# A state-space scan and window attention in one kernel: a column-grouped convolution, and the scan's products in two slots a tile

## The chip, the cores and the metric

The kernel runs on one core of one Trainium2 chip. The metric is the device time of one execution in microseconds (us), as the median of several runs. TensorE (PE) does matrix products, VectorE (DVE) and ScalarE (ACT) elementwise work, GpSimd (POOL) elementwise work on SBUF, and SyncE (SP) issues DMAs; ACT issues some too. All data are 32-bit floats.

## The reference, cut to what matters

The input is 8 images of 192 channels, 64 x 64. Layer 0 is a two-dimensional selective scan, layer 1 window attention with an MLP.

```python
# layer 0
x = conv1x1(x, W_in)                                  # 192 -> 384 channels
x = conv3x3_depthwise(x, W_dw) + b_dw                 # one 3 x 3 filter per channel
p = conv1x1(x, W_xd)                                  # 16 channels
ws, Ls, Us, Ds = (conv1x1(p, w) for w in (W_w, W_l, W_u, W_d))
xs = [x, x.T, flip(x), flip(x.T)]                     # four directions
Gl, Gm, Gr = ws / (|Gl| + |Gm| + |Gr| + eps)
for step in range(8):                                 # within chunks of 8 columns
    h = L * x + Gl * shift_up(h) + Gm * h + Gr * shift_down(h)
out = h * U + xs * D
y = sum over directions (w_m[d] * out[d])
y = conv1x1(grn(layernorm2d(y)), W_out)               # 384 -> 192
# layer 1
s = layer_norm(y as tokens)
q, k, v = s @ qkv_w.T                                 # windows of 8 x 8, 6 heads of 32
attn = l2n(q) @ l2n(k).T * temperature
attn = softmax(keep the 16 largest of each row + bias)
x2 = s + (attn @ v) @ proj_w.T
out = x2 + gelu(layer_norm(x2) @ fc1.T) @ fc2.T
```

## The kernel before

Three streams work on three images at once. `front` makes the convolved input of image b+1, `scan` runs the scan of image b, `windows` does the attention and MLP of image b-1. `side_by_side` (L716) takes a step of whichever stream is furthest behind its share; the build's scheduler then fixes one static order for each engine. Each engine takes its instructions in that order, so an instruction that waits holds all behind it on the same engine. The first front runs alone, and so do the last image's windows.

*Front (L208).* For each of 3 groups of 128 channels and each of 8 strips of 8 rows: SP loads the strip (`xt`), two products with `w_in` make `pin` (L223), ACT copies it to one of three padded strips `xin`, with two more small copies for the rows that neighbouring strips share (L226 to L232). The 3 x 3 filter is then nine products of a 128 x 128 diagonal matrix (`diag`, loaded from DRAM per channel group) with a shifted view of the strip, summed in PSUM (L242). ACT reads the sum twice, in two layouts (`st`, `sn`), and issues both stores (`xs`, `xsT`).

*Scan (L260).* Per image 8 steps t; per step 4 directions x 3 channel groups = 12 tiles of 128 channels x 512 positions; 768 tiles in all, of which 672 have gates (t > 0). `project` (L288) is a product with only 32 rows, rows 32r to 32r+31 of the weights and of `xe` or `xo`, which hold the 16-channel proxy four times over. Per tile, `first` makes the three gates `g` (three PSUM banks, row groups 0 to 2), then `pl` (L, row group 3), which DVE multiplies with the input `xv` to `lx` (L319); then D, which DVE multiplies to `dx` (L323); `second`, called one tile later, makes U, which DVE multiplies with the new state to `hu` (L360). L, D and U take turns in the single bank `u_ps`. The state update runs over ACT (absolute values L330, L331; Ln and Exp L345, L346), POOL (L341, L347, L348, L350) and DVE (L334 or L336 for gates times state, L342, L349, L351, L352). POOL adds the outputs to `y3` (L363 to L371). After 12 tiles `norm` (L373) does the layer norm of the step and stores `z`. `proxy` (L275) prepares the next step's input.

*Windows (L466).* Per image 8 rows of 8 windows: output projection (L494), transposes (L475), q, k, v, the products of the attention, the top-16 search on DVE, softmax (three wide POOL operations, L598, L599, L604), projection, MLP (L678, L679, L689).

PSUM has eight banks: `g_ps` 3, `n_ps` 1 (the denominators `nb`), `u_ps` 1 (L, D, U), `f_ps` 1 (front, proxy, norm), `l_ps` 2 (windows).

Of the kernel before, what the change touches and what calls it, by code (L numbers as in the profile page):

```python
# [17 lines left out]
F32 = mybir.dt.float32  # L18
# [7 lines left out]
P = 128  # L26
# [13 lines left out]
NEG = -100.0  # L40
LN_EXP = "natural_log_exp_and_others"
# [8 lines left out]
def tile_ss2d_then_window_attention(ctx: ExitStack, tc: tile.TileContext, a: dict, out: bass.AP):  # L50
# [31 lines left out]
    w_dw = load("w_dw")  # L82
# [30 lines left out]
    xin = [blank(f"xin{k}", [P, 10, W + 2], 0.0) for k in range(3)]  # L113

    sT, oT, xT = (blank(n, [HALF + 1, 2, GT]) for n in ("sT", "oT", "xT"))
    for t in (sT, oT, xT):
        nc.vector.memset(t[HALF : HALF + 1, 1, :], 1.0)

    dram = ctx.enter_context(tc.tile_pool(name="dram", bufs=2, space=DRAM))
    diag_d = dram.tile([CT, P, 9 * P], F32, name="diag_d", bufs=1)  # L120


    with tc.tile_pool(name="prep", bufs=2) as prep, tc.tile_pool(name="prep_ps", bufs=2, space=PSUM) as prep_ps:
        for ct in range(CT):
            dg = prep.tile([P, 9, P], F32, name="diag")
            for k in range(9):
                nc.vector.tensor_scalar(dg[:, k, :], ident, w_dw[:, ct, k : k + 1], None, ALU.mult)
            nc.sync.dma_start(diag_d[ct], dg.rearrange("p k q -> p (k q)"))

        for d in range(ND):  # L130
            rows = slice(64 * (d // 2), 64 * (d // 2) + 64)
            cols = slice((d % 2) * DIN, (d % 2 + 1) * DIN)
            nc.vector.tensor_scalar(w_g2[rows, cols], w_g2[rows, cols], w_m[rows, d : d + 1], None, ALU.mult)
# [57 lines left out]
    u_ps = ctx.enter_context(tc.tile_pool(name="u_ps", bufs=1, space=PSUM))  # L191
    f_ps = ctx.enter_context(tc.tile_pool(name="f_ps", bufs=1, space=PSUM))
# [15 lines left out]
    def front(b, xs, xsT):  # L208
        xb = x[b].rearrange("(k p) h w -> p k h w", p=HALF)
        n = 0  # L210
        for ct in range(CT):
            diag = fpool.tile([P, 9, P], F32, name="diag")
            nc.sync.dma_start(diag.rearrange("p k q -> p (k q)"), diag_d[ct])
            for s in range(NG + 1):
                if s < NG:

                    prev, cur, nxt = (xin[(n + k) % 3] for k in (-1, 0, 1))
                    n += 1
                    xt = fpool.tile([HALF, 2, 8, W], F32, name="xt")
                    nc.sync.dma_start(xt, xb[:, :, 8 * s : 8 * s + 8, :])  # L220
                    pin = f_ps.tile([P, 8, W], F32, name="fp")
                    for k in range(2):
                        nc.tensor.matmul(  # L223
                            pin, lhsT=w_in[:, k, ct * P : (ct + 1) * P], rhs=xt[:, k], start=k == 0, stop=k == 1
                        )
                    nc.scalar.copy(cur[:, 1:9, 1 : W + 1], pin)  # L226
                    if s == 0:
                        nc.gpsimd.memset(cur[:, 0, :], 0.0)
                    else:
                        nc.scalar.copy(prev[:, 9, 1 : W + 1], pin[:, 0, :])  # L230
                    if s < NG - 1:
                        nc.scalar.copy(nxt[:, 0, 1 : W + 1], pin[:, 7, :])  # L232
                    else:
                        nc.gpsimd.memset(cur[:, 9, :], 0.0)
                    yield
                if s == 0:
                    continue
                strip = xin[(n - (2 if s < NG else 1)) % 3]
                pc = f_ps.tile([P, 8, W], F32, name="fp")
                for k in range(9):  # L240
                    dy, dx = divmod(k, 3)
                    nc.tensor.matmul(  # L242
                        pc, lhsT=diag[:, k, :], rhs=strip[:, dy : dy + 8, dx : dx + W], start=k == 0, stop=k == 8
                    )
                rows = slice((s - 1) * 64, s * 64)
                st = fpool.tile([P, CH, 64], F32, name="st")
                nc.scalar.activation(
                    st.rearrange("p t (i c) -> p i c t", c=CH),
                    pc.rearrange("p i (c t) -> p i c t", t=CH),
                    AF.Identity,  # L250
                    bias=b_dw[:, ct : ct + 1],
                )
                sn = fpool.tile([P, 8, W], F32, name="sn")
                nc.scalar.activation(sn, pc, AF.Identity, bias=b_dw[:, ct : ct + 1])
                nc.scalar.dma_start(xs[:, ct, :, rows], st)
                nc.scalar.dma_start(xsT[:, ct, :, rows], sn)
                yield


    def scan(b, xs, xsT, z, made):  # L260
        gx = small.tile([P, CT, CH], F32, name="gx")

# [12 lines left out]
        def proxy(t):  # L275
# [3 lines left out]
            px = f_ps.tile([P, 512], F32, name="fp")  # L279
# [8 lines left out]
        def project(dst, w, row, col, xp):  # L288
            rows = slice(RG * row, RG * row + RG)
            nc.tensor.matmul(dst, lhsT=w[rows, col : col + P], rhs=xp[rows, :], start=True, stop=True)  # L290

        def first(t, d, ct, xp, x0):
# [14 lines left out]
            if t > 0:  # L307
                g = g_ps.tile([P, 3, 512], F32, name="g")
                for r in range(3):
                    project(g[:, r, :], w_g1, r, ch, xp)  # L310
            pl = u_ps.tile([P, 512], F32, name="pl")
            project(pl, w_g1, 3, ch, xp)
            if t == 0:
                s = hid[d][ct]
                now = by(view(s, [[1, 512]], CH), d) if d % 2 == 0 else state(d, ct)
                nc.vector.tensor_mul(now, by(pl, d), xv)
            else:
                lx = spool.tile([P, 512], F32, name="lx")
                nc.vector.tensor_mul(by(lx, d), by(pl, d), xv)  # L319
            pd = u_ps.tile([P, 512], F32, name="pl")  # L320
            project(pd, w_g2, 2 * (d // 2), (d % 2) * DIN + ct * P, xp)
            dx = spool.tile([P, 512], F32, name="dx", bufs=3)
            nc.vector.tensor_mul(by(dx, d), by(pd, d), xv)  # L323
            if t == 0:
                return dx


            ab = spool.tile([P, 2, 512], F32, name="ab", bufs=1)
            nb = n_ps.tile([P, 512], F32, name="nb")
            nc.scalar.activation(ab, g[:, 0:2, :], AF.Abs)  # L330
            nc.scalar.activation(nb, g[:, 2, :], AF.Abs)  # L331
            pr = spool.tile([P, 3, 512], F32, name="pr")
            if d % 2 == 0:
                nc.vector.tensor_mul(pr, g, view(hid[d][ct], [[CH, 3], [1, 512]]))  # L334
            else:
                nc.vector.tensor_mul(  # L336
                    pr.rearrange("p r (c i) -> p r c i", c=CH),
                    g.rearrange("p r (c i) -> p r c i", c=CH),
                    view(hid[d][ct], [[1, 3], [H + 2, CH], [1, H]]),
                )  # L340
# [12 lines left out]
            return dx  # L353

        def second(t, d, ct, xp, dx, y3):

            pu = u_ps.tile([P, 512], F32, name="pl")
            project(pu, w_g2, 2 * (d // 2) + 1, (d % 2) * DIN + ct * P, xp)
            hu = spool.tile([P, 512], F32, name="hu")
            nc.vector.tensor_mul(like(hu, d), like(pu, d), state(d, ct))  # L360
            yt = y3[:, ct, :]
            if d == 0:
                nc.gpsimd.tensor_add(yt, hu, dx)  # L363
                return
            nc.gpsimd.tensor_add(dx, dx, hu)  # L365
            yt = by(yt, 0)
            if d == 2:

                nc.gpsimd.tensor_add(yt, yt, by(dx, 0))
            else:  # L370
                nc.gpsimd.tensor_add(yt, yt, dx.rearrange("p (c i) -> p i c", c=CH))  # L371

        def norm(t, y3):  # L373
            pm = f_ps.tile([P, 512], F32, name="fp")
# [5 lines left out]
            pv = f_ps.tile([P, NT], F32, name="fp")  # L380
# [17 lines left out]
            ps = f_ps.tile([P, 512], F32, name="fp")  # L398
# [14 lines left out]
        last = None  # L413
        for t in range(CH):
            x0, xe, xo = ready
            y3 = spool.tile([P, CT, 512], F32, name="y3")
            for d in (0, 2, 1, 3):
                for ct in range(CT):
                    xp = xe if d % 2 == 0 else xo
                    dx = first(t, d, ct, xp, x0)  # L420
                    if last:
                        last()
                    last = lambda *args, t=t, d=d, ct=ct, xp=xp, dx=dx, y3=y3: second(t, d, ct, xp, dx, y3)
                    yield
                if d == 1 and t < CH - 1:
                    ready = proxy(t + 1)
            last()
            last = None
            norm(t, y3)
            yield  # L430
# [9 lines left out]
        pg = f_ps.tile([P, 1], F32, name="fp")  # L440
# [16 lines left out]
        pb = f_ps.tile([1, DM], F32, name="fp")  # L457
# [8 lines left out]
    def window_row(b, g, z, wz, bz):  # L466
        def bank(name="lp"):
            return l_ps.tile([P, 512], F32, name=name)
# [272 lines left out]
def _laid_out(i):  # L741
# [8 lines left out]
    w_g1, w_g2 = z(P, ND * DIN), z(P, 2 * DIN)  # L750
# [5 lines left out]
    for r, w in enumerate([f(L0 + "W_d"), f(L0 + "W_u")]):  # L756
        for d2 in range(2):
            at = RG * (2 * d2 + r)
            w_g2[at : at + NS] = w[2 * d2 * DIN : 2 * (d2 + 1) * DIN].T
# [17 lines left out]
        "w_dw": rows(f(L0 + "W_dw").reshape(DIN, 9), P),  # L777
# [40 lines left out]
```

## Time and profile before

| | us | share of the span |
|---|---|---|
| median of 3 runs (13549.14 to 13593.06) | 13569.98 | |
| the profiled execution | 13575.18 | |
| its span | 13573.4 | 100% |
| TensorE busy | 11668.6 | 86% |
| VectorE busy | 6446.2 | 47% |
| GpSimd busy | 6160.8 | 45% |
| ScalarE busy | 4760.2 | 35% |

The mean granted TensorE clock was 0.745 of full speed. Busy times are unions of an engine's instructions. Matmuls are pipelined and their ends are modelled: "2.07 us" for two passes whose successor starts 2.00 us later means 2.00 us of use. Each 32-bit product appears as two passes. In an instruction's line, `32*128 32x512` is 32 rows by 128 columns of the array, with 512 columns streamed through.

### The profile page before, as it was taken

The numbers are of one execution on the slowest core, as the hardware profiler recorded it, in microseconds if no ns is written. First come the engines' busy times: TensorE is split into PE (matmuls) and PEld (weight loads), VectorE is DVE, ScalarE is ACT, GpSimd is POOL, SyncE is SP. The second block draws the span as 40 slices with busy tenths as digits, with TensorE's granted clock in tenths as the row PEclk, the third lists the DMA queues.
The fourth block names the chain that finished last, engine by engine and source line by source line (L and its number), as shares of the span: only waits on it lengthen the run. The fifth ranks groups of instructions, "written<-read, shape, count | busy, mean of one in ns | idle before, by whom it ended". The sixth has DMA issues, their size and how long they took to land.

```text
span 13573.4 us, 124360 instructions
## 1 busy us (share of the span) xinstructions
PE 11668.6 (86%) x44856; PEld 5651.1 (42%) x44856; DVE 6446.2 (47%) x13918; ACT 4760.2 (35%) x8105; POOL 6160.8 (45%) x5590
## 2 busy tenths in 40 slices
PE   7888888889889898988988988898888888878655
PEld 2222344444444444444444444444444444434444
DVE  0355455553555445554455535555455544565222
ACT  1233234333334333433333333443233333333222
POOL 0366445553555434554455435555345534555111
PEclk9667677777777777877777777777777776666777
DMA  3111111111111111111111111111111110000000
GB/s 86 46 50 52 47 36 43 42 39 44 42 38 45 38 40 43 40 42 42 39 41 44 38 43 41 41 43 39 43 41 38 45 34 28 28 24 26 15 11 9
DMA packets 791475, 531.26 MB, mean 39 GB/s; under 512 B 613988, under 2 KB 614567, under 8 KB 790856
## 3 DMA queue, kind: packets, MB, share of 16 engines
q1 hardware_dynamic: 390296, 420.74, 10.9%
q10 hardware_dynamic: 400560, 102.57, 3.0%
q8 instruction: 352, 5.77, 0.2%
q14 instruction: 267, 2.19, 0.1%
HBM read 345.28 MB, written 177.93 MB: 39 GB/s over the span
## 4 chain that ended last, share of the span: by engine, by line
PE 59%; POOL 17%; DVE 14%; issue 5%; ACT 5%; DMA 0%; POOLq 0%; ACTq 0%; SPq 0%; DVEq 0%
PE pl L290 12%; PE fp L242 8%; PE lp L689 6%; PE g L290 4%; PE lp L678 3%; PE lp L679 3%; PE lp L494 3%; POOL pr L350 3%; POOL pr L348 2%; PE fp L223 2%; POOL pr L347 2%; POOL dx L365 2%; PE fp L383 2%; POOL six L598 2%; PE lp L475 2%
## 5 line engine op out<-in xcount | busy, mean ns | idle before, releaser
L290 PE MATMUL pl<-xo,w_g 32*128 32x512 f32 x2304 | 1838.3, 888 | 623.4 <-DVE lx L319 429.1
L242 PE MATMUL fp<-xin,diag 128*128 128x512 f32 x3456 | 2022.9, 721 | 43.0 <-ACT xin L232 13.6
L290 PE MATMUL pl<-xe,w_g 32*128 32x512 f32 x2304 | 1776.2, 860 | 171.0 <-DVE lx L319 102.5
L341 POOL TENSOR_TENSOR ab<-ab 128x512 f32<-128x512 f32 x672 | 878.3, 1307 | 1249.1 <-ACT ab L330 1230.3
L347 POOL TENSOR_TENSOR pr<-pr 128x512 f32<-128x512 f32 x672 | 855.7, 1273 | 1206.3 <-DVE pr L334 637.5
L365 POOL TENSOR_TENSOR dx<-dx,hu 128x512 f32<-128x512 f32 x576 | 729.1, 1266 | 1364.0 <-DVE hu L360 1355.5
L242 PEld LDWEIGHTS fp<-xin,diag 128*128 128x128 f32 x3456 | 707.1, 223 | 1154.3 <-issue 1018.6
L360 DVE TENSOR_TENSOR hu<-pl,hid 128x512 f32<-128x512 f32 x768 | 528.0, 688 | 1187.8 <-PE pl L290 810.0
L290 PEld LDWEIGHTS pl<-xo,w_g 32*128 32x128 f32 x2304 | 458.9, 246 | 1392.0 <-DVE lx L319 607.5
L350 POOL TENSOR_TENSOR pr<-pr,rr 128x512 f32<-128x512 f32 x672 | 865.5, 1288 | 357.3 <-ACT rr L346 329.2
L330 ACT ACTIVATE ab<-g 128x1024 f32<-128x1024 f32 x672 | 685.9, 1021 | 867.6 <-PE pl L290 355.6
L348 POOL TENSOR_TENSOR pr<-pr 128x512 f32<-128x512 f32 x672 | 897.1, 1335 | 50.7
L689 PE MATMUL lp<-six,w_f 128*96 128x256 f32 x3072 | 836.4, 429 | 89.4 <-ACT six L681 88.3
L351 DVE SCALAR_TENSOR_TENSOR nb<-nb,pr 128x512 f32<-128x512 f32 x672 | 469.5, 699 | 934.0 <-POOL pr L350 924.7
L290 PE MATMUL g<-xe,w_g 32*128 32x512 f32 x2016 | 847.3, 839 | 8.5 <-ACT xe L283 6.2
L290 PEld LDWEIGHTS pl<-xe,w_g 32*128 32x128 f32 x2304 | 443.7, 238 | 817.6 <-issue 218.5
L290 PE MATMUL g<-xo,w_g 32*128 32x512 f32 x2016 | 768.6, 900 | 14.2 <-DVE pr L336 13.8
L345 ACT ACTIVATE rr<-nb,eps 128x512 f32<-128x512 f32 x672 | 461.4, 687 | 905.4 <-DVE nb L342 896.7
L689 PEld LDWEIGHTS lp<-six,w_f 128*96 128x96 f32 x3072 | 547.5, 184 | 431.7 <-ACT six L681 147.5
L331 ACT ACTIVATE nb<-g 128x512 f32<-128x512 f32 x672 | 395.1, 588 | 801.0 <-DVE hid L352 796.7
L336 DVE TENSOR_TENSOR pr<-g,hid 128x1536 f32<-128x1536 f32 x336 | 588.3, 1751 | 151.1 <-ACT nb L331 147.4
L323 DVE TENSOR_TENSOR dx<-pl,xd 128x512 f32<-128x512 f32 x576 | 395.6, 687 | 554.0 <-PE pl L290 517.6
(195 smaller groups left out, 19874.1 us busy)
## 6 DMA issues: line engine op xcount, KB each, us to landing
xd<-xsT SPq DMA_DIRECT2D x384, 256.0 KB, 2.6
xt<-in_x_dram SPq DMA_DIRECT2D x192, 384.0 KB, 3.6
xs<-st ACTq DMA_DIRECT2D x192, 256.0 KB, 2.6
xsT<-sn ACTq DMA_DIRECT2D x192, 256.0 KB, 3.3
xd<-xs SPq DMA_DIRECT2D x192, 256.0 KB, 2.6
x<-xs SPq DMA_DIRECT2D x64, 768.0 KB, 4.7
z<-y SPq DMA_DIRECT2D x64, 768.0 KB, 3.8
six<-z SPq DMA_DIRECT2D x64, 768.0 KB, 6.0
```

What stands on the lines that cost most here:

```text
L242: nc.tensor.matmul(pc, lhsT=diag[:, k, :], rhs=strip[:, dy : dy + 8, dx : dx + W], start=k == 0, stop=k == 8)
L290: nc.tensor.matmul(dst, lhsT=w[rows, col : col + P], rhs=xp[rows, :], start=True, stop=True)
L330: nc.scalar.activation(ab, g[:, 0:2, :], AF.Abs)
L336: nc.vector.tensor_mul(pr.rearrange("p r (c i) -> p r c i", c=CH), g.rearrange("p r (c i) -> p r c i", c=CH), view(hid[d][ct], [[1, 3], [H ...
L341: nc.gpsimd.tensor_add(ab[:, 0, :], ab[:, 0, :], ab[:, 1, :])
L347: nc.gpsimd.tensor_add(pr[:, 0, :], pr[:, 0, :], pr[:, 1, :])
L348: nc.gpsimd.tensor_add(pr[:, 0, :], pr[:, 0, :], pr[:, 2, :])
L350: nc.gpsimd.tensor_mul(pr[:, 0, :], pr[:, 0, :], rr)
L351: nc.vector.scalar_tensor_tensor(nb, nb, 2.0, pr[:, 0, :], ALU.subtract, ALU.mult)
L360: nc.vector.tensor_mul(like(hu, d), like(pu, d), state(d, ct))
L365: nc.gpsimd.tensor_add(dx, dx, hu)
L689: nc.tensor.matmul(dst, lhsT=w_f2[:, m, k * HALF : (k + 1) * HALF], rhs=hd[:, m, :], start=m == 0, stop=False)
```

## The change

*Convolution.* The strip with its zero borders is written to a padded image in DRAM (`pad`, by an ACT-issued DMA) and read back by three SP loads, one for each row offset dy, so that the three offsets stand on 3 x 32 partitions, with 4 groups of 32 channels side by side in the free dimension. One product then covers the three dy of 32 channels (96 rows x 32 columns); the three dx are summed in PSUM. Four channel groups go to four column groups of the array: 12 products a strip instead of 9. The shared-row copies, the third `xin` and the `diag` loads go.

*Scan.* `tile_of` replaces `first` and `second`. L and the three gates are issued together; D and U are 64-row products (proxy rows 0 to 63 and 64 to 127, weights laid out for it in `w_g2`), issued together. `wait_for` adds dependencies so that the first of a group waits for all that its members need: L for the readers of the previous gates, D for this tile's `lx` and the previous tile's `hu`. `u_ps` has two banks. `norm` of a step runs after the first tile of the next step.

*PSUM.* `f_ps` is gone; front, proxy and norm take turns in the two `l_ps` banks with the windows. `oT` is the same buffer as `sT`. `dx` has two buffers instead of three.

```diff
-    xin = [blank(f"xin{k}", [P, 10, W + 2], 0.0) for k in range(3)]
+    xin = [blank(f"xin{k}", [P, WS, W + 2], 0.0) for k in range(2)]
+    w_cv = blank("w_cv", [3 * RG, CT, 4, 3, RG])
...
+    pad = [dram.tile([DIN, H + 2, W + 2], F32, name=f"pad{k}", bufs=1) for k in range(2)]
...
-    u_ps = ctx.enter_context(tc.tile_pool(name="u_ps", bufs=1, space=PSUM))
-    f_ps = ctx.enter_context(tc.tile_pool(name="f_ps", bufs=1, space=PSUM))
+    u_ps = ctx.enter_context(tc.tile_pool(name="u_ps", bufs=2, space=PSUM))
     l_ps = ctx.enter_context(tc.tile_pool(name="l_ps", bufs=2, space=PSUM))
...
-            diag = fpool.tile([P, 9, P], F32, name="diag")
-            nc.sync.dma_start(diag.rearrange("p k q -> p (k q)"), diag_d[ct])
+            own = padded[ct * P : (ct + 1) * P]
...
-                    pin = f_ps.tile([P, 8, W], F32, name="fp")
+                    pin = l_ps.tile([P, 8, W], F32, name="fp", tag="lp")
...
-                    nc.scalar.copy(cur[:, 1:9, 1 : W + 1], pin)
...
+                    nc.scalar.copy(cur[:, :, 1 : W + 1], pin)
+                    nc.scalar.dma_start(own[:, 8 * s + 1 : 8 * s + 9, :], cur)
...
+                strip = fpool.tile([3 * RG, 4, WS * (W + 2)], F32, name="strip")
+                for dy in range(3):
+                    nc.sync.dma_start(
+                        strip[dy * RG : (dy + 1) * RG],
+                        own[:, 8 * (s - 1) + dy : 8 * s + dy, :].rearrange("(q m) h w -> m q (h w)", m=RG),
                     )
+                rows4 = strip.rearrange("p q (h w) -> p q h w", h=WS)
+                pc = l_ps.tile([P, 8, W], F32, name="fp", tag="lp")
+                for dx in range(3):
+                    for q in range(4):
+                        nc.tensor.matmul(
+                            pc[q * RG : (q + 1) * RG],
+                            lhsT=w_cv[:, ct, q, dx, :],
+                            rhs=rows4[:, q, :, dx : dx + W],
+                            start=dx == 0,
+                            stop=dx == 2,
+                        )
...
+        def wait_for(ins, others):
+            for o in others:
+                tc.add_manual_dep(ins.ins, o.ins.name, DATA_READY, reason="group")
+
+        def tile_of(t, d, ct, xp, x0, y3, last):
...
             pl = u_ps.tile([P, 512], F32, name="pl")
-            project(pl, w_g1, 3, ch, xp)
+            with tc.high_priority():
+                lead = end = project(pl, w_g1, 96, RG, ch, xp)
+                if t > 0:
+                    g = g_ps.tile([P, 3, 512], F32, name="g")
+                    with tc.issue_after(lead.ins):
+                        for r in range(3):
+                            end = project(g[:, r, :], w_g1, RG * r, RG, ch, xp)
+            wait_for(lead, readers)
...
+            before = [times_l]
+            if last:
+                before.append(last())
+            pd, pu = (u_ps.tile([P, 512], F32, name="pl") for _ in range(2))
+            with tc.high_priority(), tc.issue_after(end.ins):
+                lead = project(pd, w_g2, 0, 64, ch, xp)
+                with tc.issue_after(lead.ins):
+                    project(pu, w_g2, 64, 64, ch, xp)
+            wait_for(lead, before)
+            dx = spool.tile([P, 512], F32, name="dx")
             nc.vector.tensor_mul(by(dx, d), by(pd, d), xv)
...
+                    last = tile_of(t, d, ct, xe if d % 2 == 0 else xo, x0, y3, last)
+                    if done:
+                        norm(*done)
+                        done = None
+                        yield
                     yield
```

`readers` are the two ACT reads of the gates and the DVE product of gates and state; `last()` is the previous tile's `outputs`, whose first instruction is its `hu`.

## The prediction

> **What bounds the kernel now.** I read the page's busy times and slices first. The lines are each engine's busy time with its share of the span, and the granted TensorE clock in 40 slices, in tenths.
>
> ```profile
> PE 11668.6 (86%) x44856; PEld 5651.1 (42%) x44856; DVE 6446.2 (47%) x13918; ACT 4760.2 (35%) x8105; POOL 6160.8 (45%) x5590
> PEclk9667677777777777877777777777777776666777
> ```
>
> TensorE is busy for 11668.6 of 13573.4 us and idle for 1904.8; no other engine is above half. Then the chain of work that ended last:
>
> ```profile
> PE 59%; POOL 17%; DVE 14%; issue 5%; ACT 5%; DMA 0%; POOLq 0%; ACTq 0%; SPq 0%; DVEq 0%
> PE pl L290 12%; PE fp L242 8%; PE lp L689 6%; PE g L290 4%; PE lp L678 3%; PE lp L679 3%; PE lp L494 3%; POOL pr L350 3%; POOL pr L348 2%; PE fp L223 2%; POOL pr L347 2%; POOL dx L365 2%; PE fp L383 2%; POOL six L598 2%; PE lp L475 2%
> ```
>
> The lines that the change touches, L290 (scan products) and L242 (convolution), are 24% of the chain; 41% of the chain is other engines, so the kernel is not bound by TensorE alone. Next the busy time of single lines over the whole run, each as a union (PE, then weight loads): L290, L242, and of L290 the pl tile alone.
>
> ```profile
> 0.00:13573.00 13573.00, 4106.69 (x8640) 1119.47 (x8640) 0.75 0.14 39
> 0.00:13573.00 13573.00, 2022.94 (x3456) 707.05 (x3456) 0.75 0.14 39
> 0.00:13573.00 13573.00, 3614.53 (x4608) 902.58 (x4608) 1581.61 (x2304) 0.75 0.14 39
> ```
>
> Each f32 matmul is two recorded passes: 8640 passes are 4320 products. Then the timeline, to see what runs at once:
>
> ```profile
> 6139.50 1.57 PE L533 MATMUL lp<-w_v,sT 96*128 96x192 f32 x8
> 6140.90 7.04 PE L242 MATMUL fp<-xin,diag 128*128 128x512 f32 x16
> 6147.87 0.70 PE L290 MATMUL g<-xe,w_g 32*128 32x512 f32 x3
> 6147.89 0.69 PE L290 MATMUL pl<-xe,w_g 32*128 32x512 f32 x1
> 6148.40 0.60 PE L290 MATMUL g<-xe,w_g 32*128 32x512 f32 x3
> 6148.42 0.59 PE L290 MATMUL pl<-xe,w_g 32*128 32x512 f32 x1
> 6148.94 1.08 PE L557 MATMUL lp<-ident,six 128*96 128x128 f32 x8
> 6149.95 1.12 PE L290 MATMUL pl<-xe,w_g 32*128 32x512 f32 x2
> 6151.00 1.13 PE L223 MATMUL fp<-xt,w_in 96*128 96x512 f32 x2
> ...
> 6106.45 1.90 PE L494 MATMUL lp<-wz,six 128*64 128x192 f32 x18
> 6108.28 0.54 PE L496 MATMUL lp<-bz,ones 1*64 1x192 f32 x4
> ```
>
> Four 32-row products started together at 6147.87 and took 1.07 us to the next start; one alone at 6149.95 took 1.05. So a product alone costs as much as four side by side. L494 writes two column halves in turn: 18 passes in 1.83 us, 0.102 each, where L533, as wide but in one column group, takes 1.40 / 8 = 0.175: a gain of 1.72 out of 2.
>
> Now the clock (the columns: us, busy PE, weight loads, DVE, ACT, POOL, then the clock):
>
> ```profile
> 6162.80:6190.30 27.50, 27.50 (x93) 10.66 (x92) 17.52 (x54) 8.20 (x14) 15.06 (x13) 0.50 0.09 25
> 6140.90:6147.80 6.90, 6.90 (x18) 2.84 (x16) 3.75 (x4) 1.21 (x4) 2.55 (x6) 1.00 0.00 0
> ```
>
> In the first stretch TensorE is busy throughout, mostly with 32-row products, and the clock stays at 0.50; in the second, all convolution over 128 rows, it is 1.00. A rule of the Trainium skill stands against this row: "TensorE: Matmul & The Clock Gate", Part 1, has the full clock come after some 3.4 us of sustained activity. By the rule busy time alone counts; by the row, how much of the array is in use counts as well. By the rule a shorter convolution costs clock, by the row products side by side gain some; neither enters the sum.
>
> Last, what TensorE itself waits for in the scan:
>
> ```profile
> PE pl L290 <- DVE lx L319: 531.5, 231, 8.8
> PE pl L290 <- DVE hu L360: 128.7, 133, 3.0
> PE pl L290 <- DVE dx L323: 121.4, 103, 5.3
> ```
>
> L, D and U share one bank, so each waits for the product of the one before: 781.6 us together.
>
> **The change, part by part.** *Convolution.* 192 strips x 9 products of 128 x 128 become 192 x 12 of 96 x 32, four at once in four column groups. Now: 2022.9 us for 18 passes a strip, 10.5 us a strip. After: 24 passes a strip. Bounds: none side by side, 2022.9 x 24/18 = 2697 (674 more); all four, 674. The nearest row, L494, gives 1.72 of 2, 86%; I take 86% of four, 3.44: 2697 / 3.44 = 784 us, so 1239 saved. The skill (same page, Part 3, measured speedups) has 2.38 for three column groups; by its 79%, 3.17 for four, the convolution would be 851 us and the saving 1172.
>
> *Scan.* 768 tiles x 3 single products (L, D, U) take 3614.5 / 2304 = 1.57 us each; the gates add little outside them (4106.7 in all). After: two slots a tile, L with the gates, and D with U. 1536 x 1.57 = 2410, so 1697 saved. That four row groups run at once is in the timeline; that two 64-row ones do is not shown for 512 columns. If they don't, 768 x 1.57 = 1206 comes back. I take them as together, being the same division of rows, only coarser.
>
> TensorE's busy time becomes 11668.6 - 1239 - 1697 = 8733, at an unchanged clock. The middle slices have 0.6 to 0.8: at 0.8 for the mean of 0.745 it would be 8132, at 0.6 10843. Of the two effects, shorter full-array bursts and fuller scan slots, I let neither win.
>
> *Waits of the scan.* The single bank's 781.6 us go. New: D and U wait for lx and for the previous tile's hu; L and the gates wait for all three readers of the gates and for dx in the bank. A wait here holds all that stands behind it in TensorE's queue: window and convolution matmuls, and through them ACT's copies. The loop through these waits goes from one tile's state to that of two tiles on: hu 0.69, D/U slot 1.57, dx 0.69, L slot 1.57, abs 1.02, POOL add 1.31, add 0.69, Ln 0.69, Exp 0.63, POOL product 1.29, two DVE steps 1.40: 11.5 us for two tiles, 5.8 a tile, without queues. TensorE's work is 8733 / 768 = 11.4 us a tile, so the loop hides as long as queues don't double it. They do at times: the softmax puts POOL operations of 3.44, 2.80 and 2.76 us ahead of the scan's. Bounds: 781.6 saved to 2 us more a tile, 1536. I take 500 more.
>
> *Banks.* Front, proxy and norm lose their own bank and take turns in the window's two. A window row holds both from its first L494 until the DVE has read them (L501), which needs a chain of small ACT and POOL steps: in the timeline TensorE had nothing from 6111.2 to 6117.7, 6.5 us. The cover was the front's own bank. Bounds: 0 to 64 x 6.5 = 416; I take 200. The norm (64 times, three banks in turn, each held for a DVE or ACT read of up to 1.75 us) costs 0 to 336; I take 100. It also moves one tile later, with its z store on SP's queue; the windows that read z belong to the next image, and wait only at an image's end.
>
> *Loads.* The three small copies or memsets a strip go (ACT 0.22 us each; ACT isn't the bound). In their place: 192 writes on ACT's queue and 576 strip loads on SP's, among the xd loads, against 24 diag loads. Rows of that size land in 2.6 to 3.6 us. A strip waits for its rows' write, and xd loads queue behind it; lx is late next. SP's xd loads now wait mostly for a free buffer, so there is slack, and I take 0 in the steady part; bound, one landing of some 3 us a strip, 576. In the first image the front runs alone, some 12.1 us a strip now (convolutions start at 101.10, 115.72 and 125.38). After: xt 3.6, two products 2.0, copy 0.6, write 2.6 plus 0.4 of issue: 9.2 us. That saves 2.9 of the 6.5 us counted above, so 24 x 3.6 = 86 comes back. The set-up's 27 diagonal products become a few wide ones: some us, not counted. One buffer serves as sT and oT: the next row's first transposes wait for this row's projection, which stands long before them, so nothing. The third dx buffer goes; SP's and POOL's queues keep their order there, and I count nothing.
>
> **Sum.** 8733 + 1904.8 + 500 + 300 + 86 = 11524, against the profiled execution's 13573.4 us span (13575.18 in all, 5 us above the median of the runs, 13569.98, so the same number serves for both). Check from the chain: L242's 8% and L290's 16%, cut by 61% and 41%, leave 13573 - 665 - 892 = 12016; TensorE's busy time with idle time unchanged gives 10638. Between these lies 11.5 ms. I say 11500.
>
> **The rivals.**
> *Full relief:* the idle time doesn't grow: 10638. For it: POOL and DVE are at 45% and 47%, and would be at 58% and 61%. Against: 41% of the chain is theirs already.
> *The groups don't run side by side in full:* the D/U pair one after the other gives 11524 + 1206 = 12730; the column groups in turn, 11524 + 1913 = 13437. For it: no row shows four column groups of 96 rows. Against: L494 and the gates.
> *The joined waits take over (slower):* each D/U slot stands at the head of TensorE's queue until hu of the tile before is done, which needs its whole gate chain. At 5 us a tile in place of the 0.65 I took (500 / 768): 11524 + 768 x 4.35 = 14865. It decides from 0.65 + 2049 / 768 = 3.3 us a tile. For it: lx waits reached 8.8 us, and TensorE takes its queue in order. Against: hu waits are 1.0 us on average now.
> *Little change:* gain and waits cancel, 13570.
>
> **How the numbers follow.** Forecast 0.60, its own range 10900 to 12200; full relief 0.12; groups in part 0.14; joined waits 0.11; little change 0.03. Over 0.3% (about what a measurement of this kernel can tell from no change) faster: 0.60 + 0.12 + 0.14 = 0.86; same 0.03; slower 0.11. The range leaves out the joined waits and the far ends: 10600 to 12750.
>
> **What would show it.** Convolution near 4.1 us a strip, 12 products starting four at a time; scan products near 2400 us, with four, then two, at one start; TensorE's idle time near 2.8 ms, under DVE's hu and tok. Wrong if pl waits for hu come to over 2500 us, if the column groups start one after another, or if the clock falls below 0.65.

## The result and the profile after

The changed kernel took 14201.6 us (median of 4, 14159.48 to 14238.86) against 13573.68 for the kernel before: slower, by a ratio of 1.0463 (95% interval 1.0427 to 1.0498). Forecast was 11500 us.

The page of the profiled execution (14186.5 us): busy times, granted clock in 40 slices, and the shares of the chain that ended last.

```profile
PE 9353.7 (66%) x46008; PEld 4819.9 (34%) x46008; DVE 6419.1 (45%) x13892; ACT 4722.4 (33%) x7769; POOL 6210.2 (44%) x5542
PEclk6666677667777677777777677776677767676677
...
PE 43%; DVE 22%; POOL 19%; ACT 8%; issue 5%; DMA 2%; ACTq 0%; POOLq 0%; DVEq 0%; SPq 0%
```

TensorE's busy time fell by 2315 us, from 11668.6, and yet the span grew: its idle time went from 1904.8 to 4832.8 us, 2928 more. The mean clock fell from 0.745 to 0.708. On the chain, TensorE's share fell from 59% to 43%; VectorE's grew from 14% to 22%, ACT's by 3 points, POOL's and the DMAs' by 2 each.

Busy time of single lines over the whole run, for the scan's products (L307) and the convolution (L254), and two places of the timeline:

```profile
0.00:14186.00 14186.00, 2508.15 (x8640) 651.48 (x8640) 0.71 0.20 51
...
0.00:14186.00 14186.00, 903.12 (x4608) 173.36 (x4608) 0.71 0.20 51
...
6010.85 1.13 PE L307 MATMUL pl<-xo,w_g 64*128 64x512 f32 x4 [2.87 <-DVE hu L396]
6011.91 0.98 PE L660 MATMUL lp<-six,tok 64*32 64x64 f32 x50
...
6046.40 4.69 PE L254 MATMUL fp<-strip,w_cv 96*32 96x512 f32 x24 [0.46 <-ACT xT L515]
6051.02 0.70 PE L715 MATMUL lp<-xT,w_f 96*128 96x256 f32 x2
```

The products do run side by side: D and U, four passes, take 1.06 us to the next start, where two passes of one product took 1.05 before; the 24 passes of a strip take 4.62. The saved work is real, and the idle time ate more than was saved. What each engine waited for, TensorE first (total, times, longest):

```profile
PE pl L307 <- DVE hu L396: 1601.5, 462, 14.3
PE lp L650 <- POOL six L641: 663.4, 49, 29.2
PE lp L726 <- ACT six L718: 387.9, 121, 6.1
PE pl L307 <- DVE dx L374: 352.4, 228, 10.7
...
DVE y L414 <- PE fp L413: 1538.0, 63, 46.2
DVE tok L538 <- POOL ss L217: 1281.1, 61, 49.5
```

The largest entry looks like the joined waits that the prediction had named as a rival: D and U stand at the head of TensorE's queue until hu of the tile before is done. The experiments show that it is not what made the kernel slower than the one before. The last two lines are the ones to look at: VectorE waits 1538 us for the norm's mean and 1281 us for the factors that normalize a window row. Together these two waits grew by 1811 us; in the kernel before they were:

```profile
DVE tok L501 <- POOL ss L205: 560.7, 50, 49.5
...
DVE y L377 <- PE fp L376: 447.8, 57, 17.9
```

One such place in the timeline of the changed kernel, on VectorE and, last, TensorE's line for the product that L414 waits for:

```profile
6038.72 0.69 DVE L344 TENSOR_TENSOR lx<-pl,x 128x512 f32<-128x512 f32 x1 [0.95 <-PE g L307]
...
6049.54 0.70 DVE L387 SCALAR_TENSOR_TENSOR nb<-nb,rr 128x512 f32<-128x512 f32 x1 [1.42 <-ACT rr L384]
6095.79 1.39 DVE L538 SCALAR_TENSOR_TENSOR tok<-lp,ss,n_g 128x192 f32<-128x192 f32 x4 [45.55 <-POOL ss L217]
6104.85 1.75 DVE L414 TENSOR_TENSOR y<-y,fp 128x1536 f32<-128x1536 f32 x1 [7.67 <-PE fp L413]
6106.53 1.75 DVE L354 TENSOR_TENSOR pr<-g,hid 128x1536 f32<-128x1536 f32 x1
...
6102.01 2.81 PE L413 MATMUL fp<-y,mean 128*128 128x512 f32 x6
```

and the busy times in that hole (us, then busy PE, weight loads, DVE, ACT, POOL, the clock):

```profile
6050.30:6095.70 45.40, 35.47 (x184) 25.39 (x176) 0.00 (x0) 18.08 (x28) 0.93 (x5) 0.91 0.23 50
```

The gates of the second tile of a step were ready by 6038.7. Their product with the state (L354) ran at 6106.5. In between, VectorE did nothing at all for 45 us, and POOL was busy for only 0.93 of them, while TensorE and ACT worked through the windows' MLP. Two instructions stand ahead of L354 in VectorE's queue: L538, which reads the next window row from the shared banks, and L414, which reads the norm's mean. The norm's input was complete when POOL's last L407 of the step before ended, at 6036.6, yet its product L413 ran 65 us later, after a strip of the convolution, the MLP (L715 to L730) and the next window row (L531) had had their turns in the two `l_ps` banks. L538 waited for that window row, which came after the same MLP; in this place its wait is the longer one, 45.55 us against 7.67. The scan stands still meanwhile.

### The profile page after: what moved, and what is told of

Its sections match the earlier page's. It is cut to its first block, busy times and chain, and to the rows that moved or that the text cites. A ratio compares the mean times of both kernels' runs of the same rounds, so it can differ in the third digit from the quotient of the medians.

```text
span 14186.5 us, 129799 instructions
## 1 busy us (share of the span) xinstructions
PE 9353.7 (66%) x46008; PEld 4819.9 (34%) x46008; DVE 6419.1 (45%) x13892; ACT 4722.4 (33%) x7769; POOL 6210.2 (44%) x5542
## 4 chain that ended last, share of the span: by engine, by line
PE 43%; DVE 22%; POOL 19%; ACT 8%; issue 5%; DMA 2%; ACTq 0%; POOLq 0%; DVEq 0%; SPq 0%
PE pl L307 9%; PE lp L726 6%; POOL pr L388 4%; PE lp L715 3%; PE fp L254 3%; PE lp L716 3%; DVE nb L389 2%; POOL dx L401 2%; DVE hid L390 2%; PE lp L531 2%; PE fp L420 2%; POOL pr L385 2%; DVE hu L396 2%; DVE rest L624 2%; PE fp L235 2%
## 5 line engine op out<-in xcount | busy, mean ns | idle before, releaser
L307 PE MATMUL pl<-xo,w_g 64*128 64x512 f32 (+1 forms) x2304 | 1330.0, 960 | 1498.9 <-DVE hu L396 1120.2
L307 PE MATMUL pl<-xe,w_g 64*128 64x512 f32 (+1 forms) x2304 | 1158.8, 854 | 680.8 <-DVE hu L396 481.2
L254 PE MATMUL fp<-strip,w_cv 96*32 96x512 f32 x4608 | 903.1, 838 | 238.2 <-DMA strip<-pad 223.3
L307 PEld LDWEIGHTS pl<-xo,w_g 64*128 64x128 f32 (+1 forms) x2304 | 335.7, 263 | 2126.4 <-issue 1593.5
L389 DVE SCALAR_TENSOR_TENSOR nb<-nb,pr 128x512 f32<-128x512 f32 x672 | 469.8, 699 | 967.7 <-POOL pr L388 945.9
L414 DVE TENSOR_TENSOR y<-y,fp 128x1536 f32<-128x1536 f32 x64 | 112.2, 1754 | 1538.0 <-PE fp L413 1538.0
L307 PEld LDWEIGHTS pl<-xe,w_g 64*128 64x128 f32 (+1 forms) x2304 | 295.8, 236 | 1180.2 <-issue 777.0
L538 DVE SCALAR_TENSOR_TENSOR tok<-lp,ss,n_g 128x192 f32<-128x192 f32 x256 | 89.1, 411 | 1281.3 <-POOL ss L217 1281.1
L344 DVE TENSOR_TENSOR lx<-pl,xd 128x512 f32<-128x512 f32 x504 | 346.3, 687 | 684.7 <-PE g L307 680.4
L399 POOL TENSOR_TENSOR y<-hu,dx 128x512 f32<-128x512 f32 x192 | 243.0, 1265 | 910.3 <-DVE hu L396 910.3
L650 PE MATMUL lp<-ident,six 128*128 128x128 f32 x768 | 189.5, 407 | 663.4 <-POOL six L641 663.4
L407 POOL TENSOR_TENSOR y<-y,dx 128x512 f32<-128x512 f32 x384 | 610.4, 1590 | 27.2
```

Source lines behind the costliest of these rows:

```text
L254: nc.tensor.matmul(pc[q * RG : (q + 1) * RG], lhsT=w_cv[:, ct, q, dx, :], rhs=rows4[:, q, :, dx : dx + W], start=dx == 0, stop=dx == 2,)
L307: return nc.tensor.matmul(dst, lhsT=w[rows, col : col + P], rhs=xp[rows, :], start=True, stop=True)
L389: nc.vector.scalar_tensor_tensor(nb, nb, 2.0, pr[:, 0, :], ALU.subtract, ALU.mult)
```

## The experiments

Theories, as lettered in the expectations: J, the joined waits for hu; B, the loss of the bank for front, proxy and norm; N, the norm's turn in the shared banks stops the scan; C, the convolution's loads; K, how much of the array is in use counts for the clock; S, busy time alone sets it.

**The parts one by one.** `conv_only` is the kernel before with the new convolution (and oT in sT's buffer, for room).

> The kernel before with the column-grouped convolution alone (padded image in DRAM, strip loads, 12 products in column groups; sT and oT share a buffer for room); the scan and the five PSUM pools as before. If the joined waits of the scan are what costs (theory J), the convolution alone is a gain: its busy time falls from 2023 to some 900 us and most of the difference shows, 12600 to 13100. If the loss of the front's own bank costs (theory B), the same 12600 to 13100. If the convolution's loads cost (theory C: strips late, TensorE waits for them), 13500 or more, with over 200 us of waits of the convolution for its strips.

13814.21 us, 1.0167 (1.0151 to 1.0182): slower by 1.7%, where J and B had both expected a gain. C's time came true, but the convolution's waits for its strips are 184.9 us, below C's 200. TensorE's busy time fell by only 27 us, though the convolution took 888 us less:

```profile
PE 11641.1 (84%) x46008; PEld 5377.5 (39%) x46008; DVE 6449.6 (47%) x13892; ACT 4716.6 (34%) x7769; POOL 6137.7 (44%) x5542
...
L254 PE MATMUL fp<-strip,w_cv 96*32 96x512 f32 x4608 | 1134.6, 921 | 204.0 <-DMA strip<-pad 184.9
```

The clock fell from 0.745 to 0.666; the scan's products, the same as before, rose from 4106.7 to 4658.8 us. So what the convolution saved went into the other products, and the kernel is slower by the idle time of TensorE, which grew from 1904.8 to 2166.7 us. This is taken up below (`conv_wide`).

`scan_only` is the changed kernel with the old convolution.

> The changed kernel with the nine-product convolution of before; scan in two slots and two PSUM banks for the rest as in the change. J: slower than before, 14300 to 15000, with over 1400 us of waits of D/U for hu, since these waits don't depend on the convolution. B: the same range, but the waits for hu are not what grows; those of front and window matmuls for bank readers are. C: no slower than before, 13500 or less.

14509.76 us, 1.067 (1.0649 to 1.069). The larger loss is here, in the scan and the banks; with the new convolution beside them the kernel is 308 us faster. The time fits J and B, and C's forecast failed. The waits for hu were 1438 us, as J had it, and VectorE's for the norm's mean and the window row 1570.7 and 1383.0: this fits J, and N as well.

```diff
 def wait_for(ins, others):
-    for o in others:
-        tc.add_manual_dep(ins.ins, o.ins.name, DATA_READY, reason="group")
+    return
```

> The changed kernel without the added dependencies of wait_for: L, the gates, D and U each wait for their own bank alone (D still for the bank that hu reads, by the turns of the two banks). J: 13300 or less, as products no longer wait for the slowest reader of their group. B or C: 14050 to 14350, as after.

15664.88 us, 1.1526 (1.1509 to 1.1544): J's forecast failed by far, and so did that of B and C, 14050 to 14350. Without the joined waits many of the products start one at a time, and the scan's busy time rises from 2508 to 4820.7 us. Given the rest of the change, the joins are worth 1463 us.

**The banks.** `own_bank` gives front, proxy and norm a bank again; the room comes from nb, which goes to SBUF.

```diff
-    n_ps = ctx.enter_context(tc.tile_pool(name="n_ps", bufs=1, space=PSUM))
+    f_ps = ctx.enter_context(tc.tile_pool(name="f_ps", bufs=1, space=PSUM))
...
-                nb = n_ps.tile([P, 512], F32, name="nb")
+                nb = spool.tile([P, 512], F32, name="nb", bufs=1)
```

> The changed kernel with a bank of its own for front, proxy and norm again (f_ps); to make room, the denominators nb stand in SBUF instead of PSUM, and xe has one buffer. B: 13300 or less, with the waits of convolution and norm behind window banks gone. J or C: 14000 to 14400.

13643.01 us, 1.0041 (1.0026 to 1.0055): 559 us less than the changed kernel, though VectorE was busy for 1041 us more, as its operations on nb slowed. That is not below B's 13300, but neither is it in the range of J and C, 14000 to 14400. It moved three users at once, so the next run, `norm_bank`, moves one, the norm, to the bank of nb:

```diff
-            pm = l_ps.tile([P, 512], F32, name="fp", tag="lp")
+            pm = n_ps.tile([P, 512], F32, name="fp", tag="nb")
...
-            pv = l_ps.tile([P, NT], F32, name="fp", tag="lp")
+            pv = n_ps.tile([P, NT], F32, name="fp", tag="nb")
...
-            ps = l_ps.tile([P, 512], F32, name="fp", tag="lp")
+            ps = n_ps.tile([P, 512], F32, name="fp", tag="nb")
```

> The changed kernel with the norm's three PSUM tiles in the bank of the denominators nb instead of the two shared banks; nothing else. If the scan stops at each step's end because the norm's mean waits its turn behind the windows' MLP banks, with the read of it standing ahead of the scan in VectorE's queue (theory N), the wait of L414 for L413 falls from 1538 to under 500 us and the time to 13500 or less. If the joined waits for hu (J) or the windows' own waits for banks cost (B), 13950 or more.

13271.11 us, 0.9772 (0.9753 to 0.979) of the kernel before: 930 us less than the changed kernel. It takes back all that the change had lost, and 303 us more, as N had forecast. VectorE's two waits:

```profile
DVE tok L538 <- POOL ss L217: 495.4, 58, 49.5
...
DVE y L414 <- PE fp L413: 295.6, 36, 15.8
```

The norm's mean no longer waits behind the MLP, and the longer wait for the window row goes with it. Between the two profiled executions lie 910 us; 551 of them are idle time of TensorE and 359 busy time, at a clock of 0.737 against 0.708. The scheduler's order differs on every engine between these kernels, so what the bank does cannot be told apart from the order that it brings. TensorE still waits 1265.7 us for hu: the joined waits are there in a kernel that beats the one before.

`norm_now` puts the norm back to its step's end and leaves the banks shared.

> The changed kernel with the norm at its step's end, as before the change, instead of one tile into the next step; banks shared as in the change. If the delay makes the stop (part of theory N), 13700 or less and the L413 wait well under 1538 us. If the shared banks make it, within 2% of after.

14085.39 us, 1.0376 (1.0361 to 1.0392), with 1496.1 us of waiting for the norm's mean: it stays within 2% of the changed kernel, as was expected if the banks make the stop. Without the delay by a tile the kernel is 116 us faster, no more. `banks_only` makes the bank edit alone in the kernel before.

> The kernel before with front, proxy and norm in the two window banks and no other edit (its scan, its convolution, one bank for L, D and U; one bank stays unused). B or N: slower than before by 500 us or more, with a wait of the norm's first read (L376's mean) of over 1000 us against 448. J: within 2% of before.

14256.89 us, 1.0501 (1.0485 to 1.0516): the shared banks cost 5% with the old scan and the old convolution as well. But the wait for the norm's mean was only 502.7 us, not the 1000 expected; there the scan's single bank waits more (TensorE for lx 832.6 us, against 531.5). That the sharing costs is shown for both kernels; that it acts by what stands ahead of the scan in VectorE's queue is seen in the changed one alone.

**The wait for hu.** `late_u` issues U one tile later, beside D of the next tile, with a bank of its own, so that the pair waits for the hu of two tiles ago.

```diff
-            pd, pu = (u_ps.tile([P, 512], F32, name="pl") for _ in range(2))
+            pd = u_ps.tile([P, 512], F32, name="pl")
+            pu = u_ps.tile([P, 512], F32, name="pu") if last else None
...
-            wait_for(lead, before)
+            wait_for(lead, [times_l] + products)
```

> The changed kernel with U issued one tile later: the pair is D of this tile and U of the tile before; L and D share one bank, U has the other, so the pair waits for hu of two tiles ago. If the joined waits for hu are what costs (theory J), TensorE's waits for hu fall from 1600 to under 600 us and the time to 13400 or less. If what costs is the loss of the front's own bank (theory B) or cover in general, over 13900 with the waits moved to other producers.

13998.95 us, 1.0299 (1.0284 to 1.0315). The waits for hu fell from 1601.5 to 127.1 us (94.8 on pl and 32.3 on pu), and 203 us came of it, where J had 13400 or less: the waits went to lx and pr.

```profile
PE pl L307 <- DVE lx L344: 825.9, 600, 9.8
...
PE pl L307 <- DVE pr L357: 549.8, 157, 12.8
...
PE pl L307 <- DVE pr L354: 350.4, 145, 6.7
...
PE pl L307 <- DVE hu L398: 94.8, 48, 2.1
```

> The same, and U issued one tile later, beside D of the next tile (as in late_u). N and J both at work: another 200 us or more below norm_bank, as late_u was 203 us below after. N alone: within 1% of norm_bank.

Both edits together: 13689.86 us, 1.0087 (1.0072 to 1.0102), 419 us slower than `norm_bank` alone; neither forecast held. Taking away the wait for hu on TensorE does not by itself make the kernel faster. Why late U hurts here was not tried; VectorE's wait for the norm's last product (L438 here, L436 in `norm_bank`) is 1014.9 us against 483.2.

**The clock.** `wide_du` and `narrow_du` differ in the rows of D's and U's products alone, 128 against 32, the added ones with zero weights. Instructions and order are the same on every engine.

```diff
-            project(pd, w_g2, 0, d * DIN + ct * P, xp, RG)
+            project(pd, w_g2, 0, d * DIN + ct * P, xp, P)
...
-            project(pu, w_g2, 0, (ND + d) * DIN + ct * P, xp, RG)
+            project(pu, w_g2, 0, (ND + d) * DIN + ct * P, xp, P)
```

> Control for the next run: the kernel before with D's and U's weights in separate halves of a larger tile (each on rows 0 to 15, zeros below), sT and oT in one buffer, xe with one and dx with two buffers; D and U are 32-row products, as before. All theories: within 1.5% of before, 13400 to 13780, clock 0.73 to 0.76.

> The control with one thing changed: D's and U's products run over all 128 rows, the added rows holding zero weights; same number of instructions, same order on every engine, same columns. If the clock is granted by how much of the array is in use (theory K), the clock rises from some 0.74 to 0.80 or more and the time falls by 3% or more, to 13100 or less. If busy time alone counts (theory S, the sustained-activity rule), same time and clock as the control within 0.5%.

The control took 13938.4 us, 1.0257 (1.0242 to 1.0273); its expectation of 1.5% failed. All its D and U products stand in row group 0, where the first gate is too, and it has fewer buffers; which of them costs was not tried. An edit that was expected to cost next to nothing thus moved this kernel by 2.6%, so differences of that size between kernels of different order, such as the 116, 203 and 308 us above, say little. The wide kernel took 13080.48, 0.9629 (0.9613 to 0.9646). Span and mean clock, control first:

```profile
core 0: 13931.1 us, clock 0.739
...
core 0: 13063.0 us, clock 0.819
```

Multiplying by zeros in rows that stood idle raises the clock by 0.08 and takes 6.2% off the time. For this kernel K is shown, and S falls.

> The kernel with the column-grouped convolution alone, and D and U as single products over 64 rows instead of 32 (zero weights in the added rows). K: the clock rises from 0.666 to 0.69 or more, the time falls from 13814 to 13600 or less, as the lost clock ate the convolution's gain. S: the same time within 1%.

14129.98 us, 1.0398 (1.0382 to 1.0413), clock 0.667: K's forecast failed for 64 rows, and so did S's, the same time within 1%. The order differs from that of `conv_only` on every engine, so this says little; why the clock did not rise was not tried. `conv_wide` takes all 128 rows in the order of `conv_only` (it sums D's and U's terms of two directions, so its outputs differ):

> The kernel with the column-grouped convolution alone, its D and U products taken over all 128 rows of the weights as they stand, so that each holds the sum of D's and U's terms of two directions (outputs differ); the same instructions in the same order on every engine as conv_only. If the clock, by the part of the array in use, ate the convolution's gain (theory K): the clock rises from 0.666 to 0.75 or more and the time falls from 13814 to 13200 or less. If the convolution's strips come late (theory C): 13650 or more.

13105.32 us, 0.9647 (0.9631 to 0.9663), 709 less than `conv_only` (13807.8 us of span at 0.666):

```profile
core 0: 13087.4 us, clock 0.763
```

Its waits for strips are the same, 183.1 us. So the clock, and not the strips, is what kept the convolution's gain from showing: with the same waits for strips and a higher clock the kernel is faster than the one before. Yet `conv_wide` is no faster than `wide_du` with the old convolution.

**Both findings in one.** `wide_norm` is `wide_du` with the norm in nb's bank:

> The kernel of before with D and U over 128 rows (as in wide_du, 13080) and the norm's three PSUM tiles in the denominators' bank, which leaves the front a bank to itself with the proxy. If the norm in the front's bank costs there too (theory N): 12900 or less. Otherwise 13000 to 13400.

13033.89 us, 0.9593 (0.9579 to 0.9608): the fastest that ran, with the old convolution and single D and U products. The norm's bank is worth 47 us there; N had expected 12900 or less, and 47 us are too little to say that the norm's turn costs anything where it shares a bank with front and proxy alone.

## Why the prediction was wrong

**The products.** Right in kind, a little off in size. The scan's products took 2508 us against 2410, the convolution 903 against 784, TensorE in all 9353.7 against 8733. Most of the difference can be put down to the clock: scaled by the mean clocks, 8733 x 0.745 / 0.708 is an estimated 9189.

**The clock.** The prediction read the right row (27.5 us of full business at 0.50) and then let "neither win". `conv_only` shows the size of what was dropped: removing 888 us of the densest work lowered the clock by 0.079 and left TensorE's busy time where it was. The fuller scan slots work the other way: `scan_only`, with the old convolution, has 0.756 against 0.745. The Trainium skill ("TensorE: Matmul & The Clock Gate", Part 1) has the full clock come after some 3.4 us of sustained activity. The measurement decides against time alone: `narrow_du` and `wide_du`, with the same order, differ in used rows alone, and their clocks are 0.739 and 0.819.

**The step that failed and turned the sign: banks, "I take 200", "I take 100".** Measured, the norm's turn alone is 930 us, where 100 was taken and 336 was the upper bound; without it the change would have been a gain of 303 us. What the front's turn costs by itself was not measured. The norm's bound was made from how long a bank is held. What was left out is the reader of the late bank: it has its place in VectorE's fixed queue, ahead of the scan's next tile, so that a bank which is late by an MLP stops VectorE, then POOL, then the scan. The question that the prediction put for TensorE, what is queued behind the waiting instruction, was not put for VectorE. It had also written that windows which read z wait only at an image's end, which is beside the point: the norm's cost was its wait for a bank, not its result.

The other bound, 416 us, rests on a misreading. From 6111.2 to 6117.7 the chain of the kernel before runs over other engines, but TensorE did not have "nothing". Its own timeline has it idle for 0.41 us there, and for most of the stretch it ran the norm's first product, in the very bank that the change took away:

```profile
6112.79 4.54 PE L376 MATMUL fp<-y,mean 128*128 128x512 f32 x6
6117.73 0.55 PE L475 MATMUL lp<-ident,tok 128*96 128x128 f32 x3 [0.41 <-DVE tok L501]
```

**The second step that failed: waits of the scan, "I take 500 more".** With the norm in nb's bank the kernel still takes 13271.11 us, 1771 above the forecast, so the norm's turn is not the whole miss. TensorE's idle time was forecast as 1904.8 + 500 + 300 + 86 = 2791; measured it was 4832.8, and 4281.5 in `norm_bank`. The waits of the scan's products for lx, hu and dx, 781.6 us before, came to 2031.0, which is 1249 more, not 500 (1546.9 in `norm_bank`). TensorE's wait for the softmax on POOL (L613 before, L650 after), for which the sum had no term, grew from 290.4 to 663.4 (1037.9 in `norm_bank`). The loop of 5.8 us a tile was too short: in the timeline of the changed kernel the states of three tiles are written 9.06 us apart (L390 at 6000.23, 6009.29 and 6018.35 in one stretch). There the product of gates and state (L357) stands behind the previous tile's state and hu in VectorE's queue, with three POOL operations behind it; the prediction's loop had neither that product, 1.76 us, nor two of the three POOL operations. How much of the rest is the longer loop and how much is front and proxy in the shared banks was not separated.

**The joined waits.** The slower rival named them at 5 us a tile with 3.3 as the point of decision. Waits for hu were 1601.5 / 768 = 2.1 us, below that point, and `norm_bank` beats the kernel before with most of them in place. So the rival had the right sign by the wrong mechanism. None of the signs that the prediction had named for being wrong appeared: waits for hu stayed below 2500 us, the column groups ran side by side, and the clock was above 0.65.

## What to carry to other kernels

When PSUM banks are merged, follow the reader of each bank that may come late, and ask what stands behind it in its own engine's queue; the time for which a bank is held is no bound on the cost: here 336 us by holding became 930. Less TensorE work is worth less than its time when it was the work that kept the clock up: check the clock. Here, filling the idle rows of the single D and U products with zero weights paid 6.2%. The longest wait in the list need not be the cause; move it away and see whether the time follows.

## What the runs showed of the hardware

Zero weights in otherwise idle rows raised the granted clock from 0.739 to 0.819 at the same instructions and order (`narrow_du`, `wide_du`), and using all rows with other weights raised it from 0.666 to 0.763 (`conv_only`, `conv_wide`).

VectorE's operations on nb were slower with nb in SBUF (`own_bank`) than in PSUM (the changed kernel): the median of L389 (a 128 x 512 operation) was 1564 ns against 700, of L387 1062 against 690, and L387's longest 3604 ns against 700. That POOL, which works on SBUF too, has a part in it was not tried.
